# A selective-scan layer handled in pairs of steps: one fill by each engine, one product with C and one burst of sums per sixteen scans

## The chip, the cores and the metric

The kernel runs on one core of one Trainium2 chip. It is one program: layer after layer of a small network, from the input in the chip's main memory to the output there. The metric is the device time of one execution in microseconds (us). A core has five instruction streams that wait for one another by semaphores only: PE (TensorE, matrix products into PSUM), DVE (VectorE), ACT (ScalarE, which also holds the function tables), POOL (GpSimd) and SP (SyncE, here the queue that starts nearly all transfers). Each stream runs its own instructions strictly in the order in which they were written down.

## What is computed

The input `x` is (3, 256, 48, 48) float32. Four layers are added to it one after the other, each on a group-normalised copy. Only the last one is touched here:

```
x = x + _L3_conv_ref(_gn(x), ...)
# inside, with D_INNER = 512, D_STATE = 16, tokens = 48*48 = 2304
xn = layer norm of the 256 channels of each token;  xz = xn @ in_proj;  x_in, z = split(xz)
u  = silu(causal convolution of x_in over 4 tokens)
dt_raw, B, C = split(u @ x_proj);  dt = softplus(dt_raw @ dt_proj + bias);  A = -exp(A_log)
# one token after the other:
hst = hst * exp(dt_t * A) + dt_t * B_t * u_t      # 512 x 16 states
y_t = sum over the 16 states of hst * C_t
y = (y + u * D) * silu(z);  out = y @ out_proj
```

## The kernel before

**Tiling.** The 2304 tokens of each of three images are cut into six chunks of 384 (`CH`), so the layer goes over 18 chunks (`todo`, counted by `at`). The 512 inner channels are four groups `m` of 128. One partition holds one of 32 channels and one of four states, so one `m` needs sixteen tracks of 384 tokens: four groups of states (`g`, two per half `h`) times four groups of channels (`q`). A **step** is (`at`, `m`, `h`): eight tracks, eight scans. There are 144 steps, eight to a chunk.

**One step**, in the order written down (lines 1800 to 1833):

- `fill` (L1705) puts dt·u·B into the state tile `hs` (128 x 2 x 4 x 385): DVE writes the half with `q` 0 and 1 from PSUM (L1711), POOL the other half from memory (L1715). The rows it spreads come by DMA (`spread`, L1673) and by a small product on PE into the one PSUM buffer `ps_r` (`spread_pe`, L1684).
- `decay` (L1732) is ACT's exp(dt·A) of one track, into one of three PSUM slots; `scan` (L1745) is DVE's running sum along one track (L1748), in place in `hs`. ACT is three tracks ahead, and a slot is free when its scan is over.
- `first_states` and `last_states` (L1720, L1726) carry the state from chunk to chunk with small copies on ACT.
- `times_c` (L1752) multiplies all of `hs` by C on POOL (L1765) into `hc`; `add_states` (L1770) lets PE add it up: u·D first when `h` is 0 (L1777), then eight products with a folding matrix (L1782), into the one PSUM buffer `ps_y`.
- `gate` (L1787) multiplies the sum by silu(z) on DVE.

`hs` has three buffers, `hc` two, `ps_r` and `ps_y` one each.

**Work in between.** While one chunk is scanned, the next ones are prepared and the previous one is projected out. This is written out by hand in `plan`, `after` and `gating` (lines 1373 to 1420): each entry is (half of a step `j` from 0 to 15, place, which chunk, what). Four scans make one `j`, so `m` 0 has `j` 0 to 3, `m` 1 has 4 to 7, and so on. `run` (L1422) calls the entries at four places: MID after the second scan of a `j`, DONE after the third, LATE and PE_ after the fourth. `keep_order` (L1849) then fixes the order on PE, DVE, ACT and POOL; SP is left free. The entries that matter below:

- `taps` (L1261): the convolution, eight products per `m` (`j` 0, 1, 3, 4; L1264); `take_u` (L1270) takes each from PSUM.
- `project_z` (L1339) at `j` 14, 15 and 0, and `take_z` (L1346) at 15, 0 and 1; `silu` (L1277) at 3 for z and at 7 for u, each with two loads of a function table.
- `project_y` (L1351) and `store` (L1364) of the chunk before at `j` 5, 6 and 8: the store of half 0 stands at `j` 6 and waits for that product.
- `project_dt`, `softplus`, `take_dt`, `keep_dt` (L1307 to L1337) at `j` 8 to 12.
- `group_scale`, `less_mean`, `centre`, `square_mean`, `inverse_root`, `normalise` (L1210 to L1246) at 12 to 15, two chunks ahead, and `tokens` (L1248) at 0.

`bank` is two PSUM buffers shared by all these products, so each product waits until the previous content of its bank has been taken.

Of the kernel before, what the change touches and what calls it, by code (L numbers as in the profile page):

```python
# [83 lines left out]
def net(  # L84
# [1041 lines left out]
    def w3_rooms():  # L1126

        block = upools[0].tile([P, 6, 3, CT, 256], F32, name="u")
        block = block.rearrange("p a b c d -> p (a b c d)")
        w3v.update(divide(  # L1130
            block, ("w3sb", P, (NW3,)), ("wtap", P, (DCONV, CT, DI * P)), ("dtsb", DTR + 1, (DI * P,)),
            ("amat", P, (DI * DS,)), ("rep", P, (4, 32)), ("less", P, (2, P)), ("zero", P, (8,)),
            ("xn0", P, (CT, CH + DCONV - 1)), ("xn1", P, (CT, CH + DCONV - 1)),
        ))
        rooms["xn"] = [w3v["xn0"], w3v["xn1"]]
        pieces = [wst.tile([P, 3 * 256], F32, name="wconv") for _ in range(6)]
        halves = [t.rearrange("p (t n) -> p t n", t=2) for t in pieces]
        for name, got in zip(("xg", "sq", "ot"), (halves[:2], halves[2:3], halves[3:5])):
            rooms[name] = got
        rooms["dbc"] = [halves[5][:96, j, :] for j in range(2)]  # L1140
# [92 lines left out]
    def centre(k):  # L1233
        for ct in range(CT):
            nc.scalar.copy(k.xg[:, ct, :], bank[ct])
        k.sq = room(k, "sq")
        nc.scalar.activation(k.sq, k.xg, AF.Square)
# [77 lines left out]
    def softplus(k, m0):  # L1315

        both = k.dt[:, m0 : m0 + 2, :]
        for j in range(2):
            nc.scalar.activation(k.dt[:, m0 + j, :], bank[j], AF.Abs)
        nc.scalar.activation(both, both, AF.Exp, scale=-1.0)  # L1320
        nc.scalar.activation(both, both, AF.Ln, bias=1.0)
# [42 lines left out]
    def store(k, mo):  # L1364
# [11 lines left out]
        (14, MID, 2, centre),  # L1376
# [3 lines left out]
        (0, MID, 1, lambda k: k.at > 1 and tokens(k)),  # L1380
# [12 lines left out]
        (9, LATE, 1, lambda k: softplus(k, 0)),  # L1393
        (10, MID, 1, lambda k: take_dt(k, 0)),
        (10, DONE, 1, lambda k: keep_dt(k, 0)),
# [21 lines left out]
        (15, MID, 1, lambda k: take_z(k, 0, 0)),  # L1417
# [238 lines left out]
    with ExitStack() as l3:  # L1656
# [6 lines left out]
        for name in ("u", "dtu", "bc0", "bc1", "sz"):  # L1663
            rooms[name].append(wp.tile([P, 4, CH], F32, name=name))
# [8 lines left out]
        def spread(k, m):  # L1673

            dtr = scn.tile([P, 4, CH], F32, name="dtr")
            dtur = scn.tile([P, 2, CH], F32, name="dtur")
            for t, src in ((dtr, k.dtd), (dtur, k.dtud)):
                src = src[m & 2][:, m & 1, :]
                for i in range(4):
                    r = slice(32 * i, 32 * i + 32)  # L1680
                    nc.sync.dma_start(t[r], src.rearrange("(q d) n -> d q n", d=32))
            return dtr, dtur

        def spread_pe(k, m):  # L1684

            t = psr.tile([P, 2, 512], F32, name="ps_r")
            for q in range(2):
                r = slice(32 * q, 32 * q + 32)
                nc.tensor.matmul(
                    t[:, q, :CH], rep[r].rearrange("p r d -> p (r d)"), k.dtu[r, m, :],  # L1690
                    start=True, stop=True,
                )
            k.ps = t


        steps = [(at, m, h) for at in range(len(todo)) for m in range(DI) for h in range(2)]
        tiles = {}
        state = {}

        parts_of_step = [(g, q) for a in range(2) for g in range(2) for q in (2 * a, 2 * a + 1)]  # L1700
# [4 lines left out]
        def fill(s):  # L1705

            at, m, h = steps[s]
            k = chunks[at]
            hs = tiles[s]
            bb = k.bc[0][:, 2 * h : 2 * h + 2, :].unsqueeze(2).broadcast_to([P, 2, 2, CH])  # L1710
            nc.vector.tensor_tensor(  # L1711
                hs[:, :, 0:2, 1:],
                k.ps[:, :, :CH].unsqueeze(1).broadcast_to([P, 2, 2, CH]), bb, ALU.mult,
            )
            nc.gpsimd.tensor_tensor(  # L1715
                hs[:, :, 2:4, 1:],
                k.rows[m][1].unsqueeze(1).broadcast_to([P, 2, 2, CH]), bb, ALU.mult,
            )

        def first_states(s):  # L1720
            at, m, h = steps[s]
            src = zero if chunks[at].c == 0 else state[m, h]
            hs = tiles[s] = scn.tile([P, 2, 4, CH + 1], F32, name="hs", bufs=3)
            nc.scalar.copy(hs[:, :, :, 0], src.rearrange("p (g q) -> p g q", g=2))  # L1724

        def last_states(s):  # L1726
            at, m, h = steps[s]
            if chunks[at].c < NCH - 1:
                t = state[m, h] = wp.tile([P, 8], F32, name=f"hst{m}{h}")
                nc.scalar.copy(t.rearrange("p (g q) -> p g q", g=2), tiles[s][:, :, :, CH])  # L1730

        def decay(n):  # L1732

            s, part = divmod(n, 8)
            if s >= len(steps):
                return
            at, m, h = steps[s]
            g, q = parts_of_step[part]
            col = (m * 4 + 2 * h + g) * 4 + q
            nc.scalar.activation(  # L1740
                slots[n % 3][:, 1 : CH + 1], chunks[at].rows[m][0][:, q, :], AF.Exp,
                scale=amat[:, col : col + 1],
            )

        def scan(s, part):  # L1745
            g, q = parts_of_step[part]
            b = tiles[s][:, g, q, :]
            nc.vector.tensor_tensor_scan(  # L1748
                b, slots[(8 * s + part) % 3][:, : CH + 1], b, 0.0, ALU.mult, ALU.add
            )  # L1750

        def times_c(s):  # L1752
            at, m, h = steps[s]
            cb = chunks[at].bc[1][:, 2 * h : 2 * h + 2, :].unsqueeze(2)
            hc = scn.tile([P, 2, 4, CH], F32, name="hc")
            if s == len(steps) - 1:

                for g in range(2):
                    nc.vector.tensor_tensor(
                        hc[:, g], tiles[s][:, g, :, 1:],  # L1760
                        cb[:, g].broadcast_to([P, 4, CH]), ALU.mult,
                    )
                tiles[s] = hc
                return
            nc.gpsimd.tensor_tensor(  # L1765
                hc, tiles[s][:, :, :, 1:], cb.broadcast_to([P, 2, 4, CH]), ALU.mult
            )
            tiles[s] = hc

        def add_states(s):  # L1770

            at, m, h = steps[s]
            k = chunks[at]
            hc = tiles.pop(s)
            if h == 0:
                k.y_ps = psy.tile([P, 512], F32, name="ps_y")
                nc.tensor.matmul(  # L1777
                    k.y_ps[:, :CH], diag[:, m, :], k.u[:, m, :], start=True, stop=False
                )
            for g in range(2):  # L1780
                for q in range(4):
                    nc.tensor.matmul(  # L1782
                        k.y_ps[32 * q : 32 * q + 32, :CH], fold, hc[:, g, q, :],
                        start=False, stop=h == 1 and g == 1,
                    )

        def gate(at, m):  # L1787
# [4 lines left out]
        last = len(todo) - 1  # L1792
        k = chunks[0]
        k.rows = {0: spread(k, 0)}
        spread_pe(k, 0)
# [4 lines left out]
        for s, (at, m, h) in enumerate(steps):  # L1800
            if m == 0 and h == 1 and at + 2 <= last:
                fetch(at + 2)
            for part in range(8):
                j = 4 * m + 2 * h + part // 4
                scan(s, part)
                decay(8 * s + part + 3)
                if part == 0 and h == 0:
                    c, n = (at, m + 1) if m + 1 < DI else (at + 1, 0)
                    if c <= last:
                        rows = getattr(chunks[c], "rows", {})  # L1810
                        chunks[c].rows = {**rows, n: spread(chunks[c], n)}
                if part == 4 and s + 1 < len(steps):
                    first_states(s + 1)
                if part % 4 == 1:
                    run(at, j, MID)
                if part % 4 == 2:
                    run(at, j, DONE)
                if h == 1 and part == 7 and s >= 3:
                    gate(*steps[s - 3][:2])
                if part % 4 == 3:  # L1820
                    run(at, j, LATE)
                if part == 3:
                    run(at, j, PE_)
            if s + 1 < len(steps):
                fill(s + 1)
            last_states(s)
            times_c(s)
            run(at, 4 * m + 2 * h + 1, PE_)
            if s >= 1:
                add_states(s - 1)  # L1830

            if h == 0 and s + 2 < len(steps):
                spread_pe(chunks[steps[s + 2][0]], steps[s + 2][1])

        end = len(steps) - 1
# [5 lines left out]
        gate(*steps[end][:2])  # L1841
# [117 lines left out]
```

## Time and profile before

| what | us |
|---|---|
| median of three runs | 3468.61 (3467.37 to 3470.32) |
| the profiled execution | 3469.76 |
| its span, first to last instruction | 3468.0 |
| scan layer, first scan to last instruction | 2022.7 to 3468 |
| busy in the whole span: PE, DVE, ACT, POOL | 3126.8, 2945.6, 2343.4, 1431.6 |
| one chunk in the middle (2581.36 to 2660.71) | 79.35 |
| busy in it: PE, DVE, ACT, POOL | 66.7, 76.0, 59.6, 76.7 |

The page gives, for each group of equal instructions, the busy time of all, the mean of one, and the idle time of the engine just before them with the instruction that ended it. The mean of one contains some overlap with the next on the same engine; where a sum needs the distance from start to start, it is read from the timeline. The chain view follows the end of a stretch back to what released each piece.

### The profile page before, as it was taken

The page shows a single profiled execution, that of the slowest core. Times are in us where ns is not written, and L with a number is a line of the kernel's source. Part 1 is how long each engine was busy: PE and PEld are TensorE (multiplying, and loading weights), DVE is VectorE, ACT ScalarE, POOL GpSimd, SP SyncE. Part 2 cuts the span into 40 slices and gives each one's busy share as a digit, 9 for nine tenths or more (in the row PEclk, how much of TensorE's full clock was granted, in tenths as well). Part 3 has the DMA queues.
Part 4 walks back from the last instruction along what each step waited for, and adds up shares of the span by engine and source line. Part 5 has one row for each costly group of instructions (what it writes and reads, how often), then busy time and mean ns, then how long its engine had stood idle before and what let it go on. Part 6 is the DMA issues. An engine that isn't in the chain of part 4 may idle for free.

```text
span 3468.0 us, 51952 instructions
## 1 busy us (share of the span) xinstructions
PE 3126.8 (90%) x20170; PEld 1504.1 (43%) x20170; DVE 2945.6 (85%) x3234; ACT 2343.4 (68%) x3508; POOL 1431.6 (41%) x385
## 2 busy tenths in 40 slices
PE   7999999999999999879999978888888888888885
PEld 4334343443433335457777743333434433333331
DVE  4799899869899994589955479999999999999997
ACT  3788888758888884322234367777777777777774
POOL 0000000000000001110000069999999999999997
PEclk9999999999999999999999988898999999888886
DMA  4000000010000003756301235444444444544441
GB/s 184 8 10 8 8 10 8 8 42 8 8 6 8 9 8 122 263 188 216 102 33 55 62 85 122 110 113 115 101 108 107 110 112 108 119 108 112 107 110 38
DMA packets 167603, 273.95 MB, mean 79 GB/s; under 512 B 30049, under 2 KB 134561, under 8 KB 165426
## 3 DMA queue, kind: packets, MB, share of 16 engines
q1 hardware_dynamic: 154114, 250.48, 26.7%
q10 hardware_dynamic: 13232, 20.06, 1.8%
q8 instruction: 160, 2.62, 0.3%
q14 instruction: 97, 0.79, 0.1%
HBM read 223.12 MB, written 47.10 MB: 78 GB/s over the span
## 4 chain that ended last, share of the span: by engine, by line
PE 65%; DVE 23%; ACT 7%; DMA 2%; issue 2%; POOL 0%; SPq 0%; DVEq 0%; ACTq 0%; POOLq 0%
PE ps_s L637 16%; PE acc L650 14%; DVE hs L1748 13%; PE ps_g L1264 10%; PE ps_c L1513 8%; DVE hs L1711 3%; ACT ps_da L1740 2%; PE ps_s L1030 2%; PE ps_y L1782 2%; PE ps_g L1341 2%; PE ps_y L461 2%; PE ps_m L664 2%; DVE u L295 1%; PE ps_m L710 1%; PE ps_g L1355 1%
## 5 line engine op out<-in xcount | busy, mean ns | idle before, releaser
L1748 DVE TENSOR_TENSOR_SCAN hs<-ps_da,hs 128x385 f32<-128x385 f32 x1152 | 1005.7, 939 | 50.9 <-ACT ps_da L1740 32.9
L641 ACT ACTIVATE pt<-ps_s 128x1024 f32<-128x1024 f32 x972 | 942.3, 1022 | 154.8 <-PE ps_s L637 142.1
L856 DVE TENSOR_TENSOR part<-part,pt 128x2048 f32<-128x2048 f32 x396 | 906.6, 2289 | 41.3 <-ACT pt L641 18.5
L1740 ACT ACTIVATE ps_da<-dtr,u 128x384 f32<-128x384 f32 x1152 | 653.4, 581 | 310.4 <-DVE hs L1748 290.4
L163 POOL TENSOR_TENSOR rstd<-ve,mhalf 128x2 f32<-128x2 f32 (+1 forms) x26 | 16.3, 629 | 1474.2 <-DVE ve L161 1474.2
L637 PE MATMUL ps_s<-q,kt 32*128 32x512 f32 (+1 forms) x4320 | 576.5, 592 | 0.1
L650 PE MATMUL acc<-pt,vt 128*32 128x512 f32 (+1 forms) x4320 | 520.9, 561 | 0.2
L1765 POOL TENSOR_TENSOR hc<-hs,x 128x3072 f32<-128x3072 f32 x72 | 446.1, 6196 | 28.5 <-DVE hs L1748 18.5
L1513 PE MATMUL ps_c<-vt,u 128*128 128x288 f32 x1728 | 434.5, 412 | 21.0 <-DVE u L262 21.0
L1765 POOL TENSOR_TENSOR hc<-hs,bc 128x3072 f32<-128x3072 f32 x71 | 437.9, 6168 | 23.5 <-DVE hs L1748 19.3
L1264 PE MATMUL ps_g<-u 128*128 128x384 f32 x1152 | 386.7, 491 | 1.3 <-ACT u L1273 1.3
L1513 PEld LDWEIGHTS ps_c<-vt,u 128*128 128x128 f32 x1728 | 332.2, 193 | 118.5 <-issue 19.9
L1264 PEld LDWEIGHTS ps_g<-u 128*128 128x128 f32 x1152 | 215.9, 190 | 167.3 <-ACT hs L1724 10.0
L637 PEld LDWEIGHTS ps_s<-q,kt 32*128 32x128 f32 x4320 | 195.3, 183 | 199.1 <-issue 120.2
L1782 PE MATMUL ps_y<-hc,u 128*32 128x384 f32 x2304 | 245.4, 549 | 12.5 <-POOL hc L1765 12.5
L1715 POOL TENSOR_TENSOR hs<-dtur,x 128x1536 f32<-128x1536 f32 x72 | 248.6, 3454 | 6.7 <-DMA dtur<-dtud 6.7
L1715 POOL TENSOR_TENSOR hs<-dtur,bc 128x1536 f32<-128x1536 f32 x72 | 248.7, 3454 | 0.0
L650 PEld LDWEIGHTS acc<-pt,vt 128*32 128x32 f32 x4320 | 94.4, 108 | 353.4 <-issue 326.7
L1310 PE MATMUL ps_g<-wconv,u 17*128 17x384 f32 x144 | 78.7, 680 | 82.8 <-ACT x L1331 82.8
L1782 PEld LDWEIGHTS ps_y<-hc,u 128*32 128x32 f32 x2304 | 64.4, 117 | 175.3 <-issue 144.9
L321 POOL MEMSET xpad<- 128x212 f32 x12 | 5.7, 471 | 317.7 <-ACT xpad L1564 239.1
L1341 PE MATMUL ps_g<-u 128*128 128x384 f32 x288 | 114.7, 534 | 22.5 <-ACT sz L1349 12.7
(246 smaller groups left out, 3598.4 us busy)
## 6 DMA issues: line engine op xcount, KB each, us to landing
wconv<-in_we SPq DMA_DIRECT2D x144, 384.0 KB, 4.4
dtr<-dtd SPq DMA_DIRECT2D x288, 192.0 KB, 3.9
dtur<-dtud SPq DMA_DIRECT2D x288, 96.0 KB, 4.2
wconv<-xd SPq DMA_DIRECT2D x36, 384.0 KB, 4.0
x<-bcd SPq DMA_DIRECT2D x72, 192.0 KB, 6.0
dtd<-x SPq DMA_DIRECT2D x36, 384.0 KB, 2.8
bc<-bcd SPq DMA_DIRECT2D x72, 192.0 KB, 5.8
yc<-ycat ACTq DMA_DIRECT2D x18, 576.0 KB, 4.7
```

Of the source, the lines that this page charges most:

```text
L637: nc.tensor.matmul(s[:, j, cols], kt[r, mt * P : (mt + 1) * P], q[r, :n], start=True, stop=True,)
L641: nc.scalar.activation(p[:, h0 : h0 + 2, :], s, AF.Exp)
L650: nc.tensor.matmul(acc[h * HD : (h + 1) * HD, :n], vt[:, mt, g * P + h * HD : g * P + (h + 1) * HD], p[:, h, cols], start=mt == 0, stop=mt ...
L856: ): nc.vector.tensor_tensor(part, first, p, ALU.add)
L1264: nc.tensor.matmul(bank[m % 2], w3v["wtap"][:, tap, ct, m * P : (m + 1) * P], k.xn[:, ct, tap : tap + CH], start=tap == 0 and ct == 0, sto ...
L1341: nc.tensor.matmul(bank[j], w("in", ct * 512 + m * P, P), k.xn[:, ct, DCONV - 1 :], start=ct == 0, stop=ct == CT - 1,)
L1513: nc.tensor.matmul(pc[:, :HN], u[:, i, dy, ct, m * P : (m + 1) * P], vt[:, i, ct, dy * TW : dy * TW + HN], start=ct == 0 and dy == 0, stop ...
L1715: nc.gpsimd.tensor_tensor(hs[:, :, 2:4, 1:], k.rows[m][1].unsqueeze(1).broadcast_to([P, 2, 2, CH]), bb, ALU.mult,)
L1740: nc.scalar.activation(slots[n % 3][:, 1 : CH + 1], chunks[at].rows[m][0][:, q, :], AF.Exp, scale=amat[:, col : col + 1],)
L1748: nc.vector.tensor_tensor_scan(b, slots[(8 * s + part) % 3][:, : CH + 1], b, 0.0, ALU.mult, ALU.add)
L1765: nc.gpsimd.tensor_tensor(hc, tiles[s][:, :, :, 1:], cb.broadcast_to([P, 2, 4, CH]), ALU.mult)
L1782: nc.tensor.matmul(k.y_ps[32 * q : 32 * q + 32, :CH], fold, hc[:, g, q, :], start=False, stop=h == 1 and g == 1,)
```

## The change

The step becomes a **pair**: (`at`, `m`), sixteen scans. There are 72.

- `fill`: one DVE instruction and one POOL instruction of 128 x 3072 per pair, instead of two of 128 x 1536 each.
- `times_c`: one POOL instruction of 128 x 6144 per pair, instead of two of 3072. Only the last pair is cut in parts: half on POOL, two quarters on DVE.
- `add_states`: one burst of u·D and sixteen products, after the thirteenth scan of the next pair.
- `hs` has two buffers of double size; `hc` has one buffer of double size; the state copies are half as many, 16 wide.
- `gate` of pair p stands after the third scan of pair p+2, before it stood at the end of pair p+1. `spread_pe` of the next pair stands after the eighth scan, `last_states` after the second scan of the next pair.
- The eight tracks with `q` 0 and 1 are scanned first, then the eight that POOL filled.
- `softplus(0)` is cut in three pieces at `j` 9; `take_dt(0)` and `keep_dt(0)` move to later places of `j` 10; `centre` is cut in two pieces; `take_z(0)` moves from MID to DONE; `tokens` moves from `j` 0 to the end of `j` 15.
- `dtu`, `xg` and `ot` have one buffer instead of two, and the small POOL rows `dtur` use former buffers of these. The table for exp and ln is loaded at the start of the layer.

```diff
-        for name, got in zip(("xg", "sq", "ot"), (halves[:2], halves[2:3], halves[3:5])):
+        for name, got in zip(("xg", "sq", "ot", "dtur"), (halves[:1], halves[1:2], halves[2:3], halves[3:5])):
...
-        (14, MID, 2, centre),
+        (14, MID, 2, take_centred),
+        (14, DONE, 2, take_squares),
         (14, PE_, 2, square_mean),
         (15, MID, 2, inverse_root),
         (15, LATE, 2, normalise),
-        (0, MID, 1, lambda k: k.at > 1 and tokens(k)),
+        (15, LATE, 2, tokens),
...
-        (9, LATE, 1, lambda k: softplus(k, 0)),
-        (10, MID, 1, lambda k: take_dt(k, 0)),
-        (10, DONE, 1, lambda k: keep_dt(k, 0)),
+        (9, MID, 1, lambda k: take_abs(k, 0)),
+        (9, DONE, 1, lambda k: exp_of(k, 0)),
+        (9, LATE, 1, lambda k: log_of(k, 0)),
+        (10, DONE, 1, lambda k: take_dt(k, 0)),
+        (10, LATE, 1, lambda k: keep_dt(k, 0)),
...
-        (15, MID, 1, lambda k: take_z(k, 0, 0)),
+        (15, DONE, 1, lambda k: take_z(k, 0, 0)),
...
-        for name in ("u", "dtu", "bc0", "bc1", "sz"):
+        for name in ("u", "bc0", "bc1", "sz"):
...
+        pairs = [(at, m) for at in range(len(todo)) for m in range(DI)]
+        PARTS = 16
+        in_order = [(hg, 2 * a + q) for a in range(2) for hg in range(4) for q in range(2)]
...
-            bb = k.bc[0][:, 2 * h : 2 * h + 2, :].unsqueeze(2).broadcast_to([P, 2, 2, CH])
+            bb = k.bc[0].unsqueeze(2).broadcast_to([P, 4, 2, CH])
             nc.vector.tensor_tensor(
                 hs[:, :, 0:2, 1:],
-                k.ps[:, :, :CH].unsqueeze(1).broadcast_to([P, 2, 2, CH]), bb, ALU.mult,
+                k.ps[:, :, :CH].unsqueeze(1).broadcast_to([P, 4, 2, CH]), bb, ALU.mult,
             )
             nc.gpsimd.tensor_tensor(
                 hs[:, :, 2:4, 1:],
-                k.rows[m][1].unsqueeze(1).broadcast_to([P, 2, 2, CH]), bb, ALU.mult,
+                k.rows[m][1].unsqueeze(1).broadcast_to([P, 4, 2, CH]), bb, ALU.mult,
             )
...
-            hs = tiles[s] = scn.tile([P, 2, 4, CH + 1], F32, name="hs", bufs=3)
+            hs = tiles[p] = scn.tile([P, 4, 4, CH + 1], F32, name="hs")
...
+        def times_c(p, engine, lo=0, hi=4):
+            at, m = pairs[p]
+            if lo == 0:
+                sums[p] = scn.tile([P, 4, 4, CH], F32, name="hc", bufs=1)
+            n = hi - lo
+            engine.tensor_tensor(
+                sums[p][:, lo:hi], tiles[p][:, lo:hi, :, 1:],
+                chunks[at].bc[1][:, lo:hi].unsqueeze(2).broadcast_to([P, n, 4, CH]), ALU.mult,
+            )
...
+        for p, (at, m) in enumerate(pairs):
+            if m == 0 and at + 2 <= last:
+                fetch(at + 2)
+            for part in range(PARTS):
+                n, j = PARTS * p + part, 4 * m + part // 4
+                scan(n)
+                decay(n + 3)
+                if part == 0 and p < end:
+                    rows_of(p + 1)
+                if part == 1 and p:
+                    last_states(p - 1)
                 if part % 4 == 1:
                     run(at, j, MID)
+                if part == 2 and p >= 2:
+                    gate(p - 2)
                 if part % 4 == 2:
                     run(at, j, DONE)
+                if part == PARTS - 1 and p < end:
+                    first_states(p + 1)
                 if part % 4 == 3:
                     run(at, j, LATE)
-                if part == 3:
+                if part % 4 == 3 and part < PARTS - 1:
                     run(at, j, PE_)
+                if part == 7 and p < end:
+                    spread_pe(p + 1)
+                if part == 7 and p == end:
+                    times_c(p, nc.gpsimd, 0, 2)
+                if part == 12 and p:
+                    add_states(p - 1)
+            if p < end:
+                fill(p + 1)
+                times_c(p, nc.gpsimd)
+                run(at, 4 * m + 3, PE_)
+
+        gate(end - 1)
+        times_c(end, nc.vector, 2, 3)
+        times_c(end, nc.vector, 3, 4)
         k = chunks[last]
         residual(k)
         for mo in range(2):
             project_y(k, mo, 0, DI - 1)
         add_states(end)
-        gate(*steps[end][:2])
+        gate(end)
```

`softplus` and `centre` call the pieces named above one after the other, so `softplus(2)` is unchanged.

## The prediction

> **What bounds the kernel now.** I read the page first, for the engines' shares and the costliest groups. Nothing before 2019 us is touched, so only the scan layer counts, and there POOL, idle until then, is nearly as busy as DVE:
>
> ```profile
> PE 3126.8 (90%) x20170; PEld 1504.1 (43%) x20170; DVE 2945.6 (85%) x3234; ACT 2343.4 (68%) x3508; POOL 1431.6 (41%) x385
> ...
> POOL 0000000000000001110000069999999999999997
> ...
> L1748 DVE TENSOR_TENSOR_SCAN hs<-ps_da,hs 128x385 f32<-128x385 f32 x1152 | 1005.7, 939 | 50.9 <-ACT ps_da L1740 32.9
> ...
> L1765 POOL TENSOR_TENSOR hc<-hs,x 128x3072 f32<-128x3072 f32 x72 | 446.1, 6196 | 28.5 <-DVE hs L1748 18.5
> ...
> L1715 POOL TENSOR_TENSOR hs<-dtur,x 128x1536 f32<-128x1536 f32 x72 | 248.6, 3454 | 6.7 <-DMA dtur<-dtud 6.7
> ```
>
> Next the table of busy times for one chunk in the middle (columns: length, then PE, PEld, DVE, ACT, POOL), and the timeline, which repeats every 79.3 us:
>
> ```profile
> 2581.36:2660.71 79.35, 66.68 (x279) 30.82 (x277) 76.00 (x87) 59.63 (x117) 76.72 (x17) 0.89 0.46 111
> ```
>
> DVE and POOL both leave only 3 us of a chunk free. From start to start DVE has 64 scans of 0.854 (eight took 6.82), eight fills of 1.85, four gates of 0.45, two take_dt of 2.12 and one normalise of 0.86: 76.4 us. One would think that the bound is DVE or POOL. The chain of what released what in this chunk says otherwise (start, length, what):
>
> ```profile
> 2585.57 0.79 ACT sz L1349 x2
> 2586.36 0.04 issue
> 2586.40 1.56 PE ps_g L1341 x4
> 2587.96 10.32 PE ps_g L1264 x32
> 2598.28 1.43 PE ps_y L1782 x16
> 2599.71 0.84 PE ps_r L1689 x4
> 2600.56 5.36 PE ps_g L1264 x16
> 2605.92 0.65 PE ps_y L1777 x2
> 2606.56 1.43 PE ps_y L1782 x16
> 2607.99 5.36 PE ps_g L1264 x16
> 2613.35 0.65 PE ps_g L1353 x2
> 2613.99 2.59 PE ps_g L1355 x8
> 2616.59 0.02 issue
> 2616.61 0.05 ACT wconv L1365
> ```
>
> The reader sees 30 us of PE without a gap, in the half of the chunk where it convolves the next chunk. DVE's first scan of the chunk is at S = 2583.14, of m 1 at 2602.47, of m 2 at 2620.78, of m 3 at 2641.39, of the next chunk at 2662.44: the four pairs take 19.33, 18.31, 20.61 and 21.05. In m 0 DVE waits for the end of this PE row (0.31 for ps_y, 0.27 for ps_r), in m 1 ACT waits 1.35 for it with store(0) and DVE then 0.42 for the late decay. So the first half is set by PE, the second by DVE with waits for ACT.
>
> **What the change costs on each engine alone.** DVE: the rows of 128 x 768 (0.944, L1246) and 128 x 1536 (1.742, L1711) give 0.80 per 768 elements, so a fill of 3072 takes 1.60 more: 3.46 from start to start, four times 13.8 instead of 14.8. Floor 75.4, one us less. POOL: start to start the product of 3072 takes 6.12 and the fill of 1536 takes 3.41, so 1536 elements more cost 2.71: fill 6.12, product 11.54, together 17.7 a pair, 70.6 a chunk instead of 76.3. No trace row shows the large ones: the bounds are 16.3 (that slope alone) and 19.1 a pair (nothing saved). I take 17.7; below, POOL has room for either. ACT: four state copies of each kind fewer, 0.1 each from start to start: nothing on the path. PE: the same products.
>
> **The path, pair by pair.** I placed the changed program's instructions, in the order in which they stand on each engine, on these durations.
>
> m 0. The PE row starts when take_z(2) is done: now at S+3.26, later S+3.36, since a state copy (0.1) stands ahead. project_z 1.56, taps(0) and taps(1) 10.32 end at S+15.24. Then spread_pe, 0.84: ps_r at S+16.1. DVE's sixteen scans and a gate would be over at S+14.1; behind the waiting fill stand all scans of m 1. It starts at S+16.13 and is the long one: S1 = S+19.59, 0.26 later than now. The fill that went had lain beside the PE row; the 1.6 us added to the other lie behind it.
>
> m 1. PE goes on: the whole burst of sums (0.65 + 2 x 1.43) to S+19.6, taps(2) and (3) 10.72, project_y 3.24, to S+33.55. store(0) stands on ACT ahead of the decay for scan 15, and from the end of the product to that scan's start the trace has 1.02 (2616.59 to 2617.61): scan 15 from S+34.57 to 35.44, fill 3.46, S2 = S+38.9, against 37.64 now: **1.26 lost in the first half**. The wait here grows to some 1.7 because DVE has no second fill to do meanwhile.
>
> m 2. The silu of u and its table loads (4.1) now lie beside the long fill, so the 0.57 stall after them goes. In return ACT's take_abs waits for project_dt and, with exp (0.88), delays decays: I get stalls of 0.1 and 0.6. 13.66 + 3.46 + 0.45 + 2.12 + 0.7 = 20.4, **0.2 won**.
>
> m 3. 13.66 + 3.46 + 2.12 + 0.45 + 0.86 = 20.55, plus normalise's wait for inverse_root. Its cover was the gate (0.45) just before it, which has moved. The wait is 0.25 if PE runs square_mean at the usual 1.39. But PE is then idle for longer before it: now a half burst (1.43) lies between less_mean and spread_pe, afterwards nothing. Now the gap is 1.3 to 2.5 in the chunks I looked at; after 2.25 the four records took 1.56, after 2.34 they took 1.95 with 2.77 for the next four, after 2.52 it was 2.31 and 2.44. The burst that goes and squares coming 1.0 earlier make the gap about 0.45 longer, so about half of the chunks become slow ones. A slow one costs 0.8 to 1.3 here and up to 0.4 more at the start of the next PE row, which now has a whole burst (3.5) between project_z(0) and (1). m 3 is 20.8 to 22.0; I take 21.25, 0.2 lost.
>
> [...]
>
> Sum: a chunk is 79.3 + 1.26 - 0.2 + 0.2 = 80.55, **1.25 longer**, in the 15 chunks 1 to 15: +18.8.
>
> The ends differ. Chunk 0 took 83.8 with 3.82 of waiting for POOL's first fill, which waits for dtur until 2026.54; later POOL needs 6.12 from there and DVE has a long fill and eight scans to do meanwhile: the wait is 2.0 and m 0 ends 2.5 earlier; the next fill takes 1.6 back, and m 1, which no PE row holds there, is 17.55 instead of 18.94: -2.4, taken as -2.5. Chunk 16 has the PE row but not the preparation: +1.0. Chunk 17 has no convolution: from its first scan to the end of its last it took 69.4; later 64 scans, three fills and four gates make 54.7 + 10.4 + 1.8 = 66.9: -2.5. After the last scan PE does one burst instead of two beside project_y: -2. Together -6. In all +12.8 on the profiled execution's 3469.76: 3482.6. The median shown is 1.15 below that execution, so I say **3481**.
>
> **Waits added.** hc has one buffer: POOL's product waits for the burst before. That delays it in m 0 to S+19.6, 5.5 after its scans; behind it on POOL stands the fill for m 2, for which DVE's ninth scan of m 2 waits, 9 us later than it is done. The DVE fill waits for the same product, which frees hs: by my table it ends 3 us or more ahead in every pair, so 19.1 for 17.7 costs nothing, and a product above 14.5 would start to cost. SP: fetch waits for tokens with its single xg and holds back dtr and dtur of m 1 until about S; they took 4 us to land and are needed at S+11: nothing, or up to 1 us a chunk if several transfers queue up. tokens on ACT waits for normalise beside the 3.46 fill: nothing.
>
> **Rivals.** (1) *Faster: DVE alone sets the time.* If the PE row started or ran some 3 us earlier, or DVE were not held by ps_r, the floor of 75.4 with 1.5 of ACT's waits would stand: 76.9 x 16, so -38 and -6: 3425. For it: DVE's 76 busy of 79.3, and that splitting softplus and centre spreads ACT's work. Against it: the chain above, and take_z at the second scan, where it was. (2) *Slower: every chunk slow on PE.* The gap before square_mean always long, project_z late by 0.4 to 1: 2.4 a chunk, +36 - 6: 3499; with the SP wait of 1 us, 3514. It decides from a gap above 2.3. (3) *Within noise:* stalls in m 2 and m 3 that I placed too strictly vanish, leaving the 1.26 less 0.5: +11 - 6 or less: 3465 to 3475. That the change does not do what it says is excluded by the order of its instructions.
>
> **Numbers.** A measurement of this kernel tells 0.2% (7 us) from no change. Forecast (3475 to 3492) 0.38; rival 2 and beyond 0.20; rival 3 0.20; rival 1 and what lies between 0.22. That is faster 0.22, same 0.20, slower 0.58. The range from 3445 to 3512 leaves out most of rival 1 and the far end of rival 2.
>
> **What would show it.** Right: L1264 followed by L1716 without a gap, DVE idle 2 before each fill of m 1, ACT idle some 2 before store(0) in m 1, POOL 17.7 of each pair busy. Wrong: a period near 77 with no DVE wait for PE (rival 1); L1229 near 2.5 with 22 us for m 3 (rival 2); DVE waiting for POOL before a fill.

## The result, and the profile after

The changed kernel takes 3503.22 us in the median of four executions (3500.19 to 3507.58); the kernel before, measured beside it, takes 3468.34 (3467.37 to 3470.32). The ratio is 1.0103, 95% interval 1.0089 to 1.0117: **slower by some 35 us**. I had said slower by 13. The profiled execution took 3507.58, its span is 3505.6.

From the page after, the engines' busy times and the two POOL instructions of a pair (columns as before: busy, mean ns of one, idle before, releaser):

```profile
PE 3109.4 (89%) x20170; PEld 1515.9 (43%) x20170; DVE 2951.3 (84%) x3162; ACT 2336.5 (67%) x3376; POOL 1413.7 (40%) x242
...
L1784 POOL TENSOR_TENSOR hc<-hs,x 128x6144 f32<-128x6144 f32 x36 | 437.0, 12140 | 60.9 <-PE ps_y L1800 43.5
...
L1745 POOL TENSOR_TENSOR hs<-wconv,bc 128x3072 f32<-128x3072 f32 x36 | 242.6, 6738 | 3.0 <-DMA dtud<-x 0.2
```

POOL has 143 instructions fewer and only 18 us less work. Two neighbouring chunks from the table of busy times, from first scan to first scan (length, then PE, PEld, DVE, ACT, POOL, granted clock):

```profile
2524.41:2605.61 81.20, 65.66 (x281) 31.50 (x279) 75.32 (x82) 60.53 (x110) 75.30 (x8) 0.87 0.46 108
2605.61:2685.55 79.94, 66.38 (x287) 32.10 (x284) 75.32 (x82) 60.49 (x111) 74.17 (x8) 0.89 0.45 110
```

PE, DVE and POOL work no more than before, ACT 0.9 us more, and DVE's 75.32 is what was worked out; but the chunks are longer, and of two kinds. The second one has, in the chain of what released what, the same PE row as before, with nothing between its pieces:

```profile
2610.60 10.32 PE ps_g L1270 x32
2620.92 0.84 PE ps_r L1716 x4
...
2640.76 2.58 PE ps_g L1371 x8
2643.34 0.65 PE ps_y L1795 x2
```

and the DVE timeline shows where DVE waits for it: 2.10 before the fill of m 1, and 1.33 before the last scan of m 1 (its decay stands on ACT behind store(0)). The first line here is normalise at the end of the chunk before, one of the longer kind; at the end of this one it waits only 0.29:

```profile
2601.28 0.95 DVE L1252 TENSOR_TENSOR wconv<-wconv,ps_g 128x768 f32<-128x768 f32 x1 [1.66 <-ACT ps_g L1248]
...
2621.88 3.36 DVE L1741 TENSOR_TENSOR hs<-ps_r,bc 128x3072 f32<-128x3072 f32 x1 [2.10 <-PE ps_r L1716]
...
2640.11 0.96 DVE L1777 TENSOR_TENSOR_SCAN hs<-ps_da,hs 128x385 f32<-128x385 f32 x1 [1.33 <-ACT ps_da L1769]
```

Cut by stages, the two profiled spans differ by 37.6 us: 8.8 before the last small DVE instruction ahead of the layer (`memset` of the slots, 2016.89 before and 2025.72 after; the difference is 8.9 already at 1671 us, in layers that the change does not touch), 13.9 from there to the first scan (5.78, now 19.71), -7.9 in chunk 0 (83.77, now 75.82), +18.0 in chunks 1 to 15 (79.45 each, now 80.65, from normalise to normalise), +0.5 in chunk 16, -0.3 in chunk 17, and +4.5 behind the last scan. The steady part is in its sum as forecast; the head and the tail are not.

At the head, the POOL lines and the DVE lines of the changed kernel, each in order of time:

```profile
2028.66 13.30 POOL L1745 TENSOR_TENSOR hs<-wconv,x 128x3072 f32<-128x3072 f32 x2
```
```profile
2028.73 6.63 DVE L215 COPY gsc<-rstd 128x2 f32<-128x2 f32 x1 [0.81 <-POOL rstd L163]
2035.28 0.15 DVE L217 SCALAR_TENSOR_TENSOR gsh<-gm,rstd 128x2 f32<-128x2 f32 x1
2035.40 6.59 DVE L1600 COPY norm<-gsc 128x2 f32<-128x2 f32 x1
```

Two copies of two columns take 6.6 us each, the length of POOL's first two fills (13.30 for both), beside which they start. The first one's wait for `rstd` (0.81) is over when it starts, and the 6.63 are its own busy time: other than I wrote at the start, one stream holds up another here without a semaphore (e1 and e8 below show that it is POOL's fill). In the kernel before they took 0.17, at 2019.90 and 2020.11, since POOL's first fill waited for its rows until 2026.54. Now those rows are fetched first (from 2013.40, the rows `dtr` from 2023.84), the fill is ready at once, and in every profile of a kernel with this head (after, e2, e3, e7, e9, e12) the copy that waits for POOL's `rstd` comes 0.07 behind the fill that POOL has queued next.

### The profile page after: what moved, and what is told of

It is laid out like the page before. It is cut to its first block, busy times and chain, and to the rows that moved or that the text cites. A ratio compares the mean times of both kernels' runs of the same rounds, so it can differ in the third digit from the quotient of the medians.

```text
span 3505.6 us, 51435 instructions
## 1 busy us (share of the span) xinstructions
PE 3109.4 (89%) x20170; PEld 1515.9 (43%) x20170; DVE 2951.3 (84%) x3162; ACT 2336.5 (67%) x3376; POOL 1413.7 (40%) x242
## 4 chain that ended last, share of the span: by engine, by line
PE 68%; DVE 19%; ACT 4%; issue 4%; DMA 3%; POOL 2%; SPq 0%; DVEq 0%; ACTq 0%; POOLq 0%
PE ps_s L637 15%; PE acc L650 14%; PE ps_g L1270 10%; DVE hs L1777 8%; PE ps_c L1532 7%; DVE hs L1741 3%; PE ps_y L1800 3%; PE ps_g L1371 2%; PE ps_s L1030 2%; PE ps_y L461 2%; PE ps_m L664 1%; DVE u L295 1%; PE ps_m L710 1%; PE ps_g L1290 1%; PE acc L528 1%
## 5 line engine op out<-in xcount | busy, mean ns | idle before, releaser
L1784 POOL TENSOR_TENSOR hc<-hs,x 128x6144 f32<-128x6144 f32 x36 | 437.0, 12140 | 60.9 <-PE ps_y L1800 43.5
L1532 PE MATMUL ps_c<-vt,u 128*128 128x288 f32 x1728 | 436.9, 414 | 20.8 <-DVE u L262 20.8
L1784 POOL TENSOR_TENSOR hc<-hs,bc 128x6144 f32<-128x6144 f32 (+1 forms) x36 | 430.7, 11965 | 44.6 <-PE ps_y L1800 43.0
L1270 PE MATMUL ps_g<-u 128*128 128x384 f32 x1152 | 381.6, 488 | 8.1 <-ACT u L1279 8.1
L1800 PE MATMUL ps_y<-hc,u 128*32 128x384 f32 x2304 | 232.0, 549 | 44.5 <-POOL hc L1784 43.3
L1745 POOL TENSOR_TENSOR hs<-wconv,bc 128x3072 f32<-128x3072 f32 x36 | 242.6, 6738 | 3.0 <-DMA dtud<-x 0.2
L1745 POOL TENSOR_TENSOR hs<-wconv,x 128x3072 f32<-128x3072 f32 x36 | 242.2, 6730 | 2.8 <-DMA dtud<-x 0.2
L1800 PEld LDWEIGHTS ps_y<-hc,u 128*32 128x32 f32 x2304 | 73.3, 121 | 200.4 <-issue 148.6
L1741 DVE TENSOR_TENSOR hs<-ps_r,bc 128x3072 f32<-128x3072 f32 x36 | 120.4, 3344 | 19.1 <-PE ps_r L1716 16.8
L1741 DVE TENSOR_TENSOR hs<-ps_r,x 128x3072 f32<-128x3072 f32 x36 | 120.3, 3343 | 16.6 <-PE ps_r L1716 16.6
```

What stands on the lines that cost most here:

```text
L1270: nc.tensor.matmul(bank[m % 2], w3v["wtap"][:, tap, ct, m * P : (m + 1) * P], k.xn[:, ct, tap : tap + CH], start=tap == 0 and ct == 0, sto ...
L1532: nc.tensor.matmul(pc[:, :HN], u[:, i, dy, ct, m * P : (m + 1) * P], vt[:, i, ct, dy * TW : dy * TW + HN], start=ct == 0 and dy == 0, stop ...
L1741: nc.vector.tensor_tensor(hs[:, :, 0:2, 1:], k.ps[:, :, :CH].unsqueeze(1).broadcast_to([P, 4, 2, CH]), bb, ALU.mult,)
L1745: nc.gpsimd.tensor_tensor(hs[:, :, 2:4, 1:], k.rows[m][1].unsqueeze(1).broadcast_to([P, 4, 2, CH]), bb, ALU.mult,)
L1784: engine.tensor_tensor(sums[p][:, lo:hi], tiles[p][:, lo:hi, :, 1:], chunks[at].bc[1][:, lo:hi].unsqueeze(2).broadcast_to([P, n, 4, CH]), ...
L1800: nc.tensor.matmul(k.y_ps[32 * q : 32 * q + 32, :CH], fold, hc[:, hg, q, :], start=False, stop=hg == 3,)
```

## The experiments

Theories. **A (row and ends):** the PE row sets the first half of a chunk (+18), and the rest is lost at the two ends, by DVE instructions that wait out a POOL instruction. **B (DVE or POOL):** the long fill on DVE, or POOL's larger instructions, cost it in every chunk. **C (clock):** square_mean at half rate in many chunks makes the loss; without it the change would gain.

All kernels were timed in five rounds beside the kernel before (3469 to 3470 in each set). Head is from the slots' memset to the first scan, chunk the mean distance of normalise over 15 chunks, both from the one profiled execution.

| kernel | median, us | ratio to before, 95% | head | chunk |
|---|---|---|---|---|
| before | 3468.34 | 1 | 5.78 | 79.45 |
| after | 3503.22 | 1.0103 (1.0089 to 1.0117) | 19.71 | 80.65 |
| e1 copies on ACT | 3494.55 | 1.0070 (1.0057 to 1.0084) | 12.98 | 80.79 |
| e2 split fill | 3519.21 | 1.0147 (1.0131 to 1.0162) | 18.11 | 81.90 |
| e3 half convolution, after | 3452.54 | 0.9950 (0.9937 to 0.9964) | 19.68 | 78.49 |
| e4 half convolution, before | 3453.59 | 0.9956 (0.9943 to 0.9970) | 6.11 | 78.97 |
| e5 plan on before | 3464.13 | 0.9984 (0.9976 to 0.9993) | 5.90 | 79.09 |
| e6 store later, before | 3459.17 | 0.9972 (0.9961 to 0.9982) | 6.20 | 78.83 |
| e7 keep PE busy | 3497.35 | 1.0083 (1.0069 to 1.0096) | 19.69 | 80.46 |
| e8 ends | 3496.74 | 1.0079 (1.0066 to 1.0093) | 6.27 | 81.91 |
| e9 store later, after | 3501.90 | 1.0094 (1.0079 to 1.0110) | 19.71 | 80.78 |
| e10 busy and ends | 3493.60 | 1.0069 (1.0055 to 1.0082) | 6.27 | 81.00 |
| e11 plan and store on before | 3455.55 | 0.9960 (0.9947 to 0.9972) | 5.90 | 78.43 |

**Half of the convolution, in both kernels (e3, e4).**

```diff
-        for tap in range(lo, hi):
+        for tap in range(2, 4):
...
-                    start=tap == 0 and ct == 0, stop=tap == DCONV - 1 and ct == CT - 1,
+                    start=tap == 2 and ct == 0, stop=tap == DCONV - 1 and ct == CT - 1,
```

> The changed kernel with two of the four taps of the convolution left out (half of its products, so u is wrong): PE has 2.6 us less for each m, 10.5 less in the first half of each chunk. Nothing else changes on DVE, ACT or POOL. Theory (the PE row sets the first half): m 0 and m 1 fall to DVE's 17.6 each, a chunk to 76 to 77, 64 us less in all, about 3440. Rival (DVE, POOL or the state buffers set the time): little change, over 3490.

> The kernel before with the same two taps left out. Theory (the PE row): it gains less than the changed kernel, since less of its other work lies behind the row: m 0 from 19.3 to 18.5, m 1 from 18.3 to 17.9, some 0.4 in m 2: 1.6 to 1.8 a chunk, 28 in all, about 3440, so that the two kernels meet. Rival (the large instructions or the buffers cost the time by themselves): both gain the same and the changed kernel stays some 35 slower.

Measured: -51 and -16 against the full kernels, and the two meet, though at 3453 and not at 3440. The chunks tell it without the head: the short row takes 0.48 off a chunk of before and 2.16 off one of after, which is then the quicker one; in chunks 1 to 15 DVE no longer waits for ps_r. In m 0 and m 1 together it takes 0.81 off before and 2.80 off after. Most of the rest lies ahead of the layer, where the convolution of the first chunks is prepared (memset at 2007.69 in both: 9.2 earlier than in before, 18.0 earlier than in after, whose 8.8 come back here). The chunk of e3 stays above the 76 to 77 expected; normalise waits 1.66 in nearly all of them, as in the slow chunks of after. So the row is what the pairs run into in the first half of a chunk: A, not B.

**The DVE fill in two halves again (e2).** The half for `hg` 2 and 3 stands behind the third scan of its own pair.

```diff
+        def fill_dve(p, lo):
...
+            nc.vector.tensor_tensor(
+                tiles[p][:, lo : lo + 2, 0:2, 1:],
+                k.ps[:, :, :CH].unsqueeze(1).broadcast_to([P, 2, 2, CH]),
+                k.bc[0][:, lo : lo + 2].unsqueeze(2).broadcast_to([P, 2, 2, CH]), ALU.mult,
+            )
...
-            nc.vector.tensor_tensor(
-                hs[:, :, 0:2, 1:],
-                k.ps[:, :, :CH].unsqueeze(1).broadcast_to([P, 4, 2, CH]), bb, ALU.mult,
-            )
+            fill_dve(p, 0)
...
+                if part == 2:
+                    fill_dve(p, 2)
```

> The changed kernel, but DVE's fill of 3072 is cut in two of 1536: one before the scans of the pair, one after its third scan. Theory (the row of PE work sets the first half of a chunk, and what lies behind the end of that row is paid in full): 1.6 us less before the first scan of m 2, at a price of some 0.25 more in m 2 and m 3 each: 1.1 a chunk less, 18 in all, about 3485. Rival (DVE's own work is the bound, so that an instruction more costs its fixed part): 64 to 72 more fills of some 0.25 make it 16 longer, about 3519.

Measured: +16, the rival's number, but not for the rival's reason. All chunks now are of one slow kind, 81.9. m 1 is as in after (19.07) and m 2 nearly so (20.23 for 20.21); m 0 (20.23 for 19.73) and m 3 (22.35 for 21.63) are longer. e8 below has the steady part of after unchanged, and where all its chunks are slow they take 81.91, with 20.37 in m 0 and 22.28 in m 3. So the +16 comes with the slow kind and not with the added fills, and gives B no support. Nor does it support my own theory: against chunks of the same kind the split gains nothing of the 1.1 expected. But both chunks (81.90 and 81.91) have, to 0.02, the length of 24 slots of the granted clock (3.413 us each, see e10 below). If the slots set that length, which no run tests alone, a difference of this size is hidden, so e2 does not decide what the split is worth by itself.

**The first output copy later, in both kernels (e6, e9).**

```diff
-        (6, LATE, -1, lambda k: store(k, 0)),
+        (7, MID, -1, lambda k: store(k, 0)),
```

> The kernel before, with the first output copy (store 0) run one scan pair later, in step 7 after scan 1 instead of at the end of step 6. Theory (VectorE stalls in m1 because this copy waits on ScalarE for the output projection and the decays of the next scans queue behind it): the stall of 0.4 to 1.0 us per chunk goes, 3452 to 3461 against 3468. Rival (the row on TensorE sets the chunk, the stall only moves): within 3 us of 3468.

> The changed kernel with the first output copy one scan pair later (step 7 after scan 1 of its four, instead of the end of step 6). Theory (in m1 the last scan waits 1.33 for a decay that stands behind this copy on ScalarE): m1 loses most of it, -0.6 to -1.2 per chunk, 3484 to 3494 against 3503. Rival (the row on TensorE that was late there is as late for the next step, or square_mean falls to half rate in all chunks as with the split fill): within 5 us of 3503.

In before it is worth 9.9 us, the size that the theory said; but from first scan to first scan m 2 is what got shorter (20.58 to 20.11), and m 1, where the stall stood, hardly changed (18.29 to 18.26). In after it is worth nothing, although ACT's wait in front of the copy falls. ACT's waits in the changed kernel, and then in e9, from 2105 to 3300 us (total us, times, longest):

```profile
ACT wconv L1381 <- PE ps_g L1371: 25.0, 15, 1.7
```
```profile
ACT wconv L1298 <- PE ps_g L1290: 10.2, 15, 0.7
ACT wconv L1381 <- PE ps_g L1371: 8.4, 15, 0.6
```

From first scan to first scan m 1 falls from 19.07 to 18.15, and m 2 grows from 20.21 to 21.14, in the mean of chunks 1 to 15: the stall that is removed returns one pair later. What is late next is take_dbc (L1298): its product on PE starts 36.2 us after the taps, against 34.3 in before, since a whole burst of sums with u·D (3.5 us) stands just ahead of it and no longer half of one. That this lateness is why the edit pays in before and not in after is read from the traces; no run tests it alone.

**The head and the tail (e1, e8).** e1 moves the copies from DVE to ACT:

```diff
-        nc.vector.tensor_copy(sc, rstd)
+        nc.scalar.copy(sc, rstd)
...
-                nc.vector.tensor_copy(keep[:, 0, :], sc)
-                nc.vector.tensor_copy(keep[:, 1, :], sh)
+                nc.scalar.copy(keep[:, 0, :], sc)
+                nc.scalar.copy(keep[:, 1, :], sh)
```

> The changed kernel, but the three small copies of the norm (L215, L1600, L1601) are made by ACT instead of DVE. In the changed kernel's trace two of them took 6.63 and 6.59 us, exactly as long as POOL's two first fills beside them, and DVE's first fill stood behind them. Theory (a small DVE copy waits for a POOL instruction that runs beside it): both copies are off DVE, the first scan comes about 13 us earlier, the time falls by 13 to about 3490. Rival (the copies waited for something else, such as the transfer of the rows, which would then hold the first fill as well): no change.

Measured: -8.7, of which the head has 6.7, half of what was expected, and the timeline of e1 says why: the instruction between the two copies, 0.15 in after, now waits in their place.

```profile
2020.12 6.60 DVE L217 SCALAR_TENSOR_TENSOR gsh<-gm,rstd 128x2 f32<-128x2 f32 x1 [0.80 <-POOL rstd L163]
```

So it is not these copies but whichever of these small DVE instructions starts beside POOL's fill. e8 moves that one as well, and changes the tail:

```diff
-        nc.vector.scalar_tensor_tensor(sh, gm, -1.0, rstd, ALU.mult, ALU.mult)
+        for ct in range(CT):
+            nc.scalar.activation(sh[:, ct : ct + 1], gm[:, ct : ct + 1], AF.Copy, scale=rstd[:, ct : ct + 1])
+        nc.scalar.mul(sh, sh, -1.0)
...
+            if p == end:
+                sums[p] = tiles[p][:, :, :, 1:]
...
-        gate(end - 1)
         times_c(end, nc.vector, 2, 3)
         times_c(end, nc.vector, 3, 4)
+        gate(end - 1)
```

> The changed kernel with its two ends mended and its steady part untouched: the small instructions of VectorE that stood beside GpSimd's first two fills (a copy of the scale, the shift, two kept copies) are run by ScalarE, and the last pair's products are written over its states, so that GpSimd's half starts without waiting for the sums before, and VectorE's two products start behind the last scan, ahead of the gate. Theory (about 13 us of the loss are the two waits of 6.6 at the start, about 4 the products at the end): 3503 - 13 - 4 = 3486, with the first scan some 13 earlier against the last untouched diagonal. Rival (the time moves to the first chunks or to the last projection): 3494 or more, the value that the copies alone gave, 3494.6.

The head came out as said: 6.27, 13.4 less. The tail did not: 29.0 from the end of the last scan, 26.7 in after. DVE's two products (two operands in memory) now take 2.91 and 7.71, each ending 1.6 behind a POOL product, and POOL's half, behind the first of them, takes 7.70 for the 6.16 in after. And the median fell by 6.5, not 17, the rival's side. In the profiled execution every chunk is of the slow kind, 81.92, though nothing in them was changed. But this is the longest of e8's six executions (3515.4, the others 3491.9 to 3500.4), with a mean granted clock of 0.924 against 0.935 to 0.941, so it does not stand for the others; their chunks can't be seen, and where the rest of the head's 13.4 went in them stays open.

**TensorE kept busy (e7), and all together (e10).**

```diff
+    def keep_busy(k):
+        for _ in range(3):
+            nc.tensor.matmul(bank[0], mean2, k.xg[:, 0, :], start=True, stop=True)
...
+        (14, PE_, 2, keep_busy),
         (14, PE_, 2, square_mean),
```

In e10 it is two products instead of three.

> The changed kernel with three idle products added on TensorE between the centring copies and square_mean (they write a bank that the next projection clears; the result is the same). Theory (10 of 17 chunks run square_mean at half rate, 2.9 us instead of 1.56, after a gap of over 4 us on TensorE, and normalise and the tokens behind it stand on the path): the long gap is cut to under 3 us, normalise waits 0.3 instead of 1.66 in every chunk, each chunk takes the 79.95 of the quick ones instead of 80.65 on average: about -10, 3493 against 3503. Rival (the alternation of chunks comes from the row on TensorE and the copies beside it, not from the clock): no gain, 3501 to 3508.

e7 gave some 6 of the 10 us, with an interval that overlaps that of after. Its chunks take 80.14 to 80.46, but for one of 83.29, with normalise waiting 0.60 to 0.81. (In after, 10 of 16 chunks run square_mean below full rate, behind gaps of 2.70 to 4.34, not all over 4 as expected.)

> The changed kernel with TensorE kept busy ahead of square_mean (two idle products, not three, which came out 0.3 too long per chunk), the small instructions at the head on ScalarE, and at the end the last products written over the states with the gate between VectorE's two. Theory (the loss of the head, 13, is real, and the ends alone came out with only 7 because every chunk then fell into the slow kind): 3497 - 5 - 13 - 3 = 3476, between 3472 and 3483, with all chunks at 79.95. Rival (what the head gives back is lost again in the chunks whatever TensorE does): 3488 or more.

Again the rival's number. e10 adds e8's head (6.27) and a tail with the gate between DVE's two products, which is a little better (24.3). But 7 of its 15 chunks are slow again, now 82.24 against 79.94. The two kinds show side by side in its PE timeline: after the same gap of 2.72 the four records of the idle products take 2.93 in one chunk and 1.56 in the next.

```profile
2172.53 2.93 PE L1231 MATMUL ps_g<-wconv,mean 128*128 128x384 f32 x4 [2.72 <-ACT wconv L1245]
```
```profile
2254.79 1.56 PE L1231 MATMUL ps_g<-wconv,mean 128*128 128x384 f32 x4 [2.72 <-ACT wconv L1245]
```

So the length of the gap alone does not decide. In the traces of before and after, every stretch of one granted clock but the last is a whole number of slots of 3.413 us, and over the whole span they all begin on one grid, to 0.01 us. The table of busy times for e8, cut into such slots, shows what else decides (PE's busy time is the first number behind the length, the granted clock the first one behind POOL's count):

```profile
2250.37:2253.78 3.41, 0.98 (x13) 0.29 (x6) 3.38 (x7) 2.36 (x5) 2.49 (x1) 1.00 0.00 0
2253.78:2257.20 3.42, 3.42 (x6) 1.85 (x7) 3.42 (x6) 2.42 (x5) 3.42 (x1) 0.50 0.73 215
2257.20:2260.61 3.41, 1.78 (x7) 0.49 (x5) 3.41 (x6) 2.82 (x6) 3.41 (x1) 1.00 1.09 212
2260.61:2264.02 3.41, 2.39 (x4) 1.49 (x5) 3.41 (x5) 2.44 (x5) 3.33 (x2) 0.50 0.45 116
2264.02:2267.44 3.42, 3.42 (x6) 1.71 (x6) 1.76 (x3) 1.81 (x4) 3.42 (x1) 0.50 0.09 33
```

Each slot has one clock, 1.00 or 0.50, and here the slots in which PE was busy for 0.98, 1.78 and 2.39 us are followed by one at 0.50, those in which it was busy throughout by one at 1.00. Counted over some 390 slots from 2060 us on in each of the profiles of before, after, e7, e8 and e10, all 198 with PE busy for under 1.2 us were followed by 0.50; from 1.2 to 2.8 us either clock followed. The slots do not move with the program: e8's chunk of 81.92 is 24 of them to within 0.01, so its gap falls on the same slot each time. C is right about the price (1.3 to 2.3 per chunk with all of square_mean at half rate), but the remedy does not hold: my products stood behind the gap, and with three of them 15 of 16 chunks ran square_mean at full rate (e7), with two 9 of 16 (e10). e8 and after, with the same steady part, also differ in it, so one profile of each kernel does not say how many chunks an edit makes slow. A version in which no chunk is slow was not found; by 79.94 for 80.65 it would be some 11 us quicker than after, still slower than before.

**The plan alone (e5, e12) and the better version (e11).**

> The kernel before with only the change's edits of the plan (softplus in three calls, the centring in two, its copies of dt and z one or two scans later, the tokens one step earlier), and its single steps of eight scans as they were. Theory (the plan is not where the time went, the pairs are): -0.2 to -0.5 per chunk, 3460 to 3465. Rival (the later squares make the gap ahead of square_mean longer, TensorE falls to half rate there, and the plan carries part of the +1.24 per chunk): 3472 to 3485.

> The changed kernel with the plan of the kernel before (the same edits undone). Theory (the pairs alone carry the loss, the plan's edits gain a few tenths per chunk with them): 3503 to 3515. Rival (the plan's later squares make the half rate of square_mean): below 3495, with normalise waiting 0.3 in every chunk.

> The kernel before with the plan's edits and the first output copy one step later, the two edits that need no pairs. Theory (both take away stalls of VectorE on ScalarE's decays, in different steps, so they add): 3459 less what the plan alone gave, 3450 to 3457. Rival (both spend the same slack of the row on TensorE): 3457 to 3465, no better than the later copy alone.

e5 has the plan's lines of the diff above on the kernel before: -5.9 against its own set, 0.35 less per chunk, as expected, so in the kernel before the plan's edits are good and carry no loss. e12, the pairs with the old plan, took 3537.44, but it does not compute the same: with one `xg` buffer the fetch of the next chunk stands ahead of the old place of `tokens`, so these read the next chunk's raw rows (in its trace one such transfer lands at 2436.15 and `tokens` reads at 2438.84). What the pairs cost without the plan therefore stays open; what the run shows is that the earlier tokens go with the buffer that was given up. e11 has e5 and e6 together: 3455.55, a ratio of 0.9960 (0.9947 to 0.9972). The two nearly add up (-14.4 against its own set, -5.9 and -9.9 alone), and this is the quickest full version here: its chunk is 78.43, and it has no pairs.

## Why the prediction was right in sign and short in size

The range and the sign held. By its own steps, with S the first scan of a chunk:

- **The PE row, m 0 and m 1: right.** S1 = S+19.59 forecast, 19.73 measured; S2 = S+38.9, measured 38.81; store(0)'s wait "some 1.7", measured 1.7. e3 and e4 show that the row causes it.
- **m 2: nearly right**, 20.4 forecast, 20.21 measured, with a stall behind take_abs of 0.28 where I had 0.7 in all: 0.37 won (before's mean is 20.58), not 0.2.
- **m 3: right in kind, too small.** I took 21.25 in 20.8 to 22.0, with half of the chunks slow. Measured: 20.92 in a quick and 22.29 in a fully slow one, 21.63 in the mean of chunks 1 to 15, so 0.57 lost and not 0.2; normalise waits 0.29 in 6 of 16 chunks, and 1.15 to 1.66 in the others. The reason that I gave, a gap that is 0.45 longer, is not the whole of it. The gaps before square_mean, at most 2.53 in before, now are up to 4.34, but one of 2.70 is followed by 2.92 for the four records and one of 2.94 by 1.56: the place on the slots decides too, and in e8 and e10 chunks are slow behind gaps of 2.64 and 2.72.
- **Sum of a chunk: right, in part by luck.** 80.55 forecast, 80.65 measured; +18.8 against +18.0. From before's mean chunk to after's, m 0 and m 1 lost 1.00 (1.26 forecast), m 2 won 0.37 and m 3 lost 0.57, so three misses of 0.2 to 0.4 cancel. A quick chunk takes 79.94, so some 10.6 of the 18.0 come with the slow chunks; in a quick one half of what the PE row costs, 1.00, is won back in m 2 and m 3.
- **POOL: mis-sized.** I took 17.7 per pair. Measured 12.14 + 6.74 = 18.9, where two steps of before cost 19.3 by the same means: hardly anything is saved. The step that failed is "1536 elements more cost 2.71", a slope between two different instructions (from the fill of 1536 to that of 3072 it is 3.29). In the chunks it costs nothing, as said. In chunk 17, which no PE row holds, DVE waits 1.03 and 1.25 for POOL, and instead of -2.5 there is -0.3.
- **"The ends differ … together -6": wrong, and this is the miss.** Head and chunk 0 together are +6.0 (+13.9 and -7.9), not -2.5. I looked at when POOL's first fill comes and not at which DVE instructions then stand beside it; e1 and e8 show that 13.4 of it are these. The gain in chunk 0 does not come from them: it stays in e8 (77.28) and e10 (75.89), where the head is short, so that part was undersized. Behind the last scan it is +4.5, not -2. The tail lines of after, and then of before, say how:

```profile
3485.66 6.16 POOL L1784 TENSOR_TENSOR hc<-hs,bc 128x3072 f32<-128x3072 f32 x1 [5.57 <-PE ps_y L1800]
3486.04 7.39 DVE L1784 TENSOR_TENSOR hc<-hs,bc 128x1536 f32<-128x1536 f32 x1
3493.35 1.75 DVE L1784 TENSOR_TENSOR hc<-hs,bc 128x1536 f32<-128x1536 f32 x1
```
```profile
3441.69 6.20 POOL L1765 TENSOR_TENSOR hc<-hs,bc 128x3072 f32<-128x3072 f32 x1
3446.16 3.34 DVE L1759 TENSOR_TENSOR hc<-hs,bc 128x1536 f32<-128x1536 f32 x1
```

POOL's half waits for the one `hc` buffer and starts 0.4 ahead of DVE's first product. That one ends 1.61 behind POOL's, as it did in before, where POOL's had only 1.7 left when it started; the next one, alone, takes 1.75. So the two take 9.06 together, 5.01 before. That the single `hc` buffer costs this is read from these lines; e8, which takes it away, only exchanged one wait for others. The ends are +10.8 in all, 16.8 more than the sum has.
- **8.8 us that are no term.** The memset lay at 2013.0 to 2025.7 in the profiled executions of after, e2, e7, e9 and e12, which share the code ahead of it; after's was the latest, and why they spread so stays open. By the medians the loss is 34.9, by the two profiled spans 37.6.
- **Rivals.** Rival 2's 3499 came nearest, by another way: not all chunks are slow in after. e2 and e8 show that its mechanism exists (81.9 per chunk, all slow). Rival 1 is excluded by DVE's wait for ps_r, and rival 3 by the result.
- **Waits added:** `hc`, the SP fetch and the tokens cost nothing in the chunks, as said; `hc` does at the end.

The head and the tail show one wait from both sides: in after a copy that took 0.17 in before takes 6.63 when it starts 0.07 behind a fill of 6.7, and DVE's product ends 1.61 behind POOL's; in e8 POOL's half takes 7.70 for 6.16 behind DVE's product. The trace of before has it at the tail: 3.34 for the product beside POOL's, 1.75 for the next one, alone. From this I could have expected a wait at the head; its size, a whole fill, is first shown by after.

## What to carry to other kernels

Fewer and larger instructions on engines that are not the bound brought nothing here; a chain on one engine (the PE row) set half of the chunk, and a few lines moved in the old plan gained 14 us while the rewriting lost 35. When a long POOL instruction comes earlier or lies elsewhere, list every small DVE instruction that may start beside it, at the head (6.6 us each here) and the tail too. And work out the ends of a loop from their own timeline, not as what is left of the steady state.

## What the runs showed of the hardware that was not expected

- DVE copies of 128 x 2 (after) and a scaled product of two such columns (e1) took as long as the POOL fill beside them (6.6 us instead of 0.15 to 0.17), while in after DVE fills of 128 x 3072 and scans, with one operand in PSUM, took 3.33 to 3.36 and 0.93 to 0.96 throughout, with POOL busy beside nearly all of them. DVE products of 128 x 1536 with both operands in memory took 1.75 alone (before and after); beside a POOL product they ended 1.6 behind its end, whether they started 1.7 ahead of that end (before, 3.34 us) or 5.8 (after, 7.39 us), and likewise in e8 (2.91 and 7.71 us). The wait goes both ways: POOL's product of 3072 took 7.70 in e8, where such a DVE product was ahead of it, instead of 6.2.
- POOL's time was nearly proportional to the elements: 3.45 (before) and 6.74 (after) for fills of 1536 and 3072, 6.2 (before) and 12.14 (after) for products of 3072 and 6144.
- In the traces of before and after the granted clock changes only between slots of 3.413 us. Two kernels settled on a chunk of whole slots: e8 on 81.92, which is 24, with square_mean at half rate in every chunk, and e3 on 78.51, which is 23, likewise.
